# A decoder layer with state-space mixing, cross attention and experts: three residual sums moved into the accumulation of the products

## The chip, the cores and the metric

The kernel runs on one core of one Trainium2 chip. The metric is the device time of one execution in microseconds (us); the time of a kernel is the median of several executions. Five engines work side by side, each through its own queue in order: TensorE (PE, with its weight loads PEld), VectorE (DVE), ScalarE (ACT), GpSimd (POOL) and SyncE (SP), which here only issues transfers (DMA).

## The reference, cut to what matters

All arrays are float32: 32 batches of 256 rows of 256 columns. Each of the three parts adds its result to its input and normalizes each row.

```python
def _layernorm(x, axis=-1, eps=1e-05):
    m = jnp.mean(x, axis=axis, keepdims=True)
    v = jnp.var(x, axis=axis, keepdims=True)
    return (x - m) / jnp.sqrt(v + eps)
...
x = _layernorm(x + _L0_attn_ref(x, ...), axis=-1)        # state-space scan, ends in  y @ W_out.T + b_out
x = _layernorm(x + _L0_xattn_ref(x, ctx, ctx, ...), axis=-1)  # 16 heads, ends in  out @ w_o.T + b_o
x = _layernorm(x + _L0_ffn_ref(x, w1, w3, w2), axis=-1)  # 8 experts by position, (silu(x w1) * (x w3)) w2
return x
```

## The kernel before, in words

**Three streams of work run interleaved.** The first goes batch by batch through the state-space layer: projections, a short convolution, and then 512 scan steps in all, 16 for a batch. A step is a product `bu` on VectorE (L631), the scan itself on VectorE (L650, 128x1024), four exponentials on ScalarE that feed it (L602), and a multiplication of its result by C on GpSimd (L666). Every four steps PE sums over the states (`y`, L680) and VectorE gates the sum (`yg`, L696). The second stream is the attention of a batch: scores for the row maxima (`tops`, L897, on VectorE), scores again with exponentials on ScalarE (L955), and sums over the values (`ps_oT`, L924). The third is the experts: the rows of eight batches, regrouped by expert, are 32 units (`expert_unit`), each with three weight matrices loaded from memory. A unit computes two hidden products (`ps_h`, L1194), gates them on VectorE (L1258) and multiplies by w2 into one bank (`ps_down`, L1273). The last eight units hold two experts each, for four batches (the pair units), so that only four of them need the last batch.

**The three sums.** The product with `w_out` (name `ps_out`, in `mixes`), the product with `w_o` (`ps_o`, in `finish`) and `ps_down` each fill one PSUM bank of 128x512 float32, two halves of 128x256. VectorE adds the residual rows from SBUF (L823, L1025, L1285) and writes the sum over them in SBUF (`x1` or `xe`; the profile calls `x1` `x`). Then `layernorm` (L338) takes that SBUF tile: for each half `bn_stats` and `bn_aggr` on VectorE (L344, L345), four operations on 128x2 numbers on GpSimd for the factor and the offset (L348 to L352), and for each half one ScalarE operation that scales and shifts the rows in place (L355). For `x1` of the first norm, b_out has been added to the rows on GpSimd before (L810), and b_o after the norm (L837). 96 such norms run: 32 for each of the three places. The second stores its rows to `x2d` in memory, from where the experts load them again (`xe<-x2d`).

**PSUM.** Two pools: one for `b_bc` and `bu` of the scan, and a ring of five banks (`RING`, tag `mm`) that all other products share. A chain asks for banks with `take(n, rank, t)`, and gives one back with `done(n, t)` after the instruction that reads it last. The units ask with the lowest rank.

**What sets the order.** The order of instructions on every engine is fixed when the program is built. `Clock` keeps an assumed time for each engine, `spend` advances it by an assumed cost (`MM`, `VE`, `EV`, `GP`), and `in_order` always advances the chain (a generator) that can start first, with a lag per chain as its preference. Chains wait for each other through these assumed times only; on the chip each engine then runs its list in order and waits for its operands. A changed cost or a changed hold of a bank therefore changes the order on all engines, far from the changed lines. The units take what the other chains leave; those that haven't found a place before the scans end are done behind them.

Of the kernel before, what the change touches and what calls it, by code (L numbers as in the profile page):

```python
# [10 lines left out]
AF = mybir.ActivationFunctionType  # L11
ALU = mybir.AluOpType
# [4 lines left out]
P = 128  # L17
B, L, D = 32, 256, 256
DI, NS, DTR = 512, 16, 64
NDC = DI // P  # L20
# [19 lines left out]
NFC = 6  # L40
# [8 lines left out]
class Clock:  # L49
# [7 lines left out]
    def spend(self, engine, us, after=0.0):  # L57

        self.at[engine] = max(self.at[engine], after, self.base) + us
        return self.at[engine] + 0.3  # L60
# [40 lines left out]
def decoder_kernel(ctx: ExitStack, tc: tile.TileContext, a: dict, out: bass.AP):  # L101
    nc = tc.nc
    clock = Clock()
    spend = clock.spend
# [9 lines left out]
    ident = cpool.tile([P, P], F32, name="ident")  # L114
# [39 lines left out]
    def weight(name, rows, cols):  # L154
        t = wp.tile([P, rows // P, cols], F32, tag=name, name=name)
        dma(t, a[name].rearrange("(k p) c -> p k c", p=P))
        return t
# [72 lines left out]
    w_out = weight("w_out", DI, D)  # L230
    w_q, b_q = heads("q", "oT")
    w_o = weight("w_o", D, D)
# [16 lines left out]
    for i in range(3):  # L249
        t = keep.tile([P, GB, NQ, L], F32, name=f"da_{i}")  # L250
# [77 lines left out]
    def bank(name):  # L328
        return ps_mm.tile([P, 2 * L], F32, tag="mm", name=name)


    MM = 0.49
    EV = {1: 0.42, 2: 0.56, 4: 1.05}
    VE = {1: 0.41, 2: 0.66, 4: 1.225}
    CV = 0.535
    GP = {1: 0.7, 2: 1.23, 4: 2.36}

    def layernorm(tiles, t):  # L338

        n = len(tiles)  # L340
        mv = small.tile([P, n, 2], F32, tag="ln_mv", name="ln_mv")
        for i, x in enumerate(tiles):
            st = small.tile([P, 6], F32, tag="ln_st", name="ln_st")
            nc.vector.bn_stats(st, x)  # L344
            nc.vector.bn_aggr(mv[:, i, :], st)  # L345
        yield spend("DVE", 0.6 * n, t), "POOL"
        rstd = small.tile([P, n, 1], F32, tag="ln_rstd", name="ln_rstd")
        nc.gpsimd.tensor_scalar_add(rstd, mv[:, :, 1:2], EPS)  # L348
        nc.gpsimd.tensor_tensor(rstd, rstd, power[:, :n, :], ALU.pow)
        off = small.tile([P, n, 1], F32, tag="ln_off", name="ln_off")  # L350
        nc.gpsimd.tensor_tensor(off, mv[:, :, 0:1], rstd, ALU.mult)
        nc.gpsimd.tensor_scalar_mul(off, off, -1.0)  # L352
        yield spend("POOL", 1.5), "ACT"
        for i, x in enumerate(tiles):
            nc.scalar.activation(  # L355
                x, x, AF.Identity, bias=off[:, i, :], scale=rstd[:, i, :]
            )
        return spend("ACT", 0.55 * n)

# [431 lines left out]
    def mixes():  # L791


        yield lambda: None if later else spread.get(0), "DVE"
        bv = unit1.tile([P, 2, P], F32, tag="x1T", name="bv")
        nc.vector.tensor_copy(bv, b_v.to_broadcast([P, 2, P]))
        yield from take(1, 1, spend("DVE", 0.3))
        ps = bank("ps_bv")
        for k in range(2):
            nc.tensor.matmul(ps[:, :D], bv[:, k, :], w_o[:, k, :], start=(k == 0), stop=(k == 1))  # L800
        yield spend("PE", 2 * MM), "DVE"
        nc.vector.tensor_tensor(b_o, ps[:, :D], b_o, ALU.add)
        done(1, spend("DVE", VE[1]))
        for b in range(B):
            if b >= 2:
                yield lambda: stored[b - 2] + 3.0 if len(stored) >= b - 1 else None, "SP"
            load_x1(b)
            yield clock.at["SP"] + LANDING, "POOL"
            x1 = x1s[b]
            nc.gpsimd.tensor_tensor(  # L810
                x1, x1, b_out.unsqueeze(1).to_broadcast([P, 2, D]), ALU.add
            )
            spend("POOL", GP[2])
            yield lambda: gated.get(b), "PE"
            yield from take(1, 1, gated[b])
            yg = ygs.pop(b)
            ps, t = product(
                "ps_out",
                lambda t: [yg[:, k, t * P : (t + 1) * P] for k in range(NDC)],
                lambda t: [w_out[:, k, :] for k in range(NDC)],  # L820
            )
            yield t, "DVE"
            nc.vector.tensor_tensor(x1, ps, x1, ALU.add)  # L823
            t = spend("DVE", VE[2])
            done(1, t)
            t = yield from layernorm([x1[:, t, :] for t in range(2)], t)
            yield lambda: None if x1Ts else t, "PE"
            yield from take(1, 2, t)
            ps, t = transposes(x1)
            yield t, "ACT"  # L830
            x1T = unit1.tile([P, 2, L], F32, tag="x1T", name=f"x1T_{b}")
            nc.scalar.copy(x1T, ps)
            t = spend("ACT", EV[2])
            done(1, t)
            x1Ts[b] = x1T, t
            yield t, "POOL"
            nc.gpsimd.tensor_tensor(x1, x1, b_o.unsqueeze(1).to_broadcast([P, 2, D]), ALU.add)  # L837
            spend("POOL", GP[2])
# [146 lines left out]
    def finish(b):  # L985
        att = unit1.tile([P, 2, H, DK], F32, tag="att", name=f"att_{b}")
        HH = H // 2
        for g2 in range(2):

            yield lambda: oSs[0][1] if oSs else None, "PE"  # L990
            yield from take(1, 2.5, oSs[0][1])
            oS = oSs[0][0]
            ps = bank("ps_oB").rearrange("p (t j n) -> p t j n", t=2, j=2)
            for n in range(2):
                for j in range(2):
                    nc.tensor.transpose(ps[:, n, j, :], oS[:, j, n * P : (n + 1) * P], ident)
            del oSs[0]
            yield spend("PE", 0.6), "DVE"
            o = ps.rearrange("p t g (j c) -> p t (g j) c", c=32)
            rec = small.tile([P, 2, HH, 1], F32, tag="rec", name="rec")  # L1000
            nc.vector.reciprocal(rec, o[:, :, :, DK : DK + 1])
            nc.vector.tensor_tensor(
                att[:, :, g2 * HH : (g2 + 1) * HH, :],
                o[:, :, :, :DK],
                rec.to_broadcast([P, 2, HH, DK]),
                ALU.mult,
            )
            t = spend("DVE", 0.7)
            done(1, t)
        x1 = ending.pop(0)  # L1010
        yield from take(1, 3, t)
        ps, t = transposes(att.rearrange("p t h d -> p t (h d)"))
        yield t, "ACT"
        aT = unit1.tile([P, 2, L], F32, tag="aT", name=f"aT_{b}")
        nc.scalar.copy(aT, ps)
        t = spend("ACT", EV[2])
        done(1, t)
        yield from take(1, 2.5, t)
        ps, t = product(
            "ps_o",  # L1020
            lambda t: [aT[:, k, t * P : (t + 1) * P] for k in range(2)],
            lambda t: [w_o[:, k, :] for k in range(2)],
        )
        yield t, "DVE"
        nc.vector.tensor_tensor(x1, ps, x1, ALU.add)  # L1025
        t = spend("DVE", VE[2])
        done(1, t)
        t = yield from layernorm([x1[:, t, :] for t in range(2)], t)
        yield t, "SP"
        dma(x2d[b].rearrange("(t p) d -> p t d", p=P), x1)  # L1030
        stored.append(t)
# [129 lines left out]
    def expert_unit(bufs, u):  # L1161
# [12 lines left out]
        xe = xes.pop(u)  # L1174
        yield from take(1, unit_rank, x_at[u])
        ps = bank("ps_xe").rearrange("p (k e n) -> p k e n", k=2, e=2)
# [40 lines left out]
        for b in range(3):  # L1217
            yield weights("w1", b), "PE"
            yield from take(1, unit_rank, max(tx, weights("w1", b)()))
            ps, t = hidden("w1", b)  # L1220
# [10 lines left out]
        def second():  # L1231
# [19 lines left out]
            for b in range(3):  # L1251
                yield weights("w3", b), "PE"
                yield from take(1, unit_rank, max(th[0] - 2, weights("w3", b)()))
                ps, t = hidden("w3", b)
# [8 lines left out]
            po = bank("ps_down").rearrange("p (e n) -> p e n", e=2)  # L1263
            for j in range(2):
                e = es[j]
                if j == 0 or pair:
                    yield lambda: max(ts, w_at[u, "w2", e]) if (u, "w2", e) in w_at else None, "PE"
                terms = [i for i in range(len(FS)) if FS[i][0] == e]
                for i in terms:
                    f = FS[i][1]  # L1270
                    m = min(P, FF - f * P)
                    cols = slice(0, P) if pair else slice(j * P, (j + 1) * P)
                    nc.tensor.matmul(  # L1273
                        po[:, j, :],
                        h[i // m_in][:m, i % m_in, cols],
                        w_tiles[u, "w2", e][f // 3][:m, f % 3, :],
                        start=(i == terms[0]),
                        stop=(i == terms[-1]),
                    )
                t = spend("PE", NFC * MM)  # L1280
                if j == 1 or pair:
                    bufs.free["w2"].append(t)
            bufs.sets.append((place, t))
            yield t, "DVE"
            nc.vector.tensor_tensor(xe, po, xe, ALU.add)  # L1285
            t = spend("DVE", VE[2])
            done(1, t)
            t = yield from layernorm([xe[:, j, :] for j in range(2)], t)
            yield t, "SP"
            for j in range(2):  # L1290
                dma(rows_of(out, u, j), xe[:, j, :])
# [111 lines left out]
```

## Time and profile before

| | |
|---|---|
| median of three runs | 2786.34 us (2783.25 to 2790.03) |
| profiled execution | 2777.42 us, its span 2775.7 us |
| busy: PE, DVE | 2354.4 us, 2381.9 us |
| busy: ACT, POOL | 2063.1 us, 1787.5 us |
| mean granted TensorE clock | 0.899 |
| L823, L1025, L1285 | 32 each, 682, 673 and 682 ns |
| L344 and L345 | 192 each, 411 and 182 ns |
| L355 (192) | 597 ns on `x`, 596 on `xe` |
| start of the last scan | 2587.8 us |
| start of the last DVE sum (L1285) | 2767.6 us |

The span reaches from the first to the last instruction. A group of the profile names the line, the engine, the operation, the tiles `out<-in` with their shapes, the count, the busy time and the mean length of one in ns, and then the idle time of the engine just before them with what ended it. A float32 product of 128x256 stands in the trace as two records. In the windows, PEclk is the granted TensorE clock as a share of full speed.

### The profile page before, as it was taken

The page shows a single profiled execution, that of the slowest core. Times are in us where ns is not written, and L with a number is a line of the kernel's source. Part 1 is how long each engine was busy: PE and PEld are TensorE (multiplying, and loading weights), DVE is VectorE, ACT ScalarE, POOL GpSimd, SP SyncE. Part 2 cuts the span into 40 slices and gives each one's busy share as a digit, 9 for nine tenths or more (in the row PEclk, how much of TensorE's full clock was granted, in tenths as well). Part 3 has the DMA queues.
Part 4 walks back from the last instruction along what each step waited for, and adds up shares of the span by engine and source line. Part 5 has one row for each costly group of instructions (what it writes and reads, how often), then busy time and mean ns, then how long its engine had stood idle before and what let it go on. Part 6 is the DMA issues. An engine that isn't in the chain of part 4 may idle for free. (4 is left out here: it accounts for less than half of the span.)

```text
span 2775.7 us, 47073 instructions
## 1 busy us (share of the span) xinstructions
PE 2354.4 (85%) x16004; PEld 1644.8 (59%) x16004; DVE 2381.9 (86%) x2413; ACT 2063.1 (74%) x4331; POOL 1787.5 (64%) x1408
## 2 busy tenths in 40 slices
PE   6688888887898988898888988888779988888988
PEld 4555555565566666566555666655456655555767
DVE  3988999999999998999998998899998999988422
ACT  7777777888778887878787877877778777765531
POOL 5877777777776766666765766666766666655200
PEclk8888898989899999999789999999888988988999
DMA  7877777787788778677676887677678766777745
GB/s 196 235 208 207 215 222 223 229 231 225 215 229 224 215 203 228 183 221 201 185 198 176 233 221 199 192 203 194 178 197 218 206 201 192 199 207 215 221 148 176
DMA packets 403396, 573.93 MB, mean 207 GB/s; under 512 B 49300, under 2 KB 234900, under 8 KB 403156
## 3 DMA queue, kind: packets, MB, share of 16 engines
q1 hardware_dynamic: 403156, 570.92, 72.9%
q8 instruction: 127, 2.08, 0.3%
q14 instruction: 113, 0.93, 0.1%
HBM read 476.92 MB, written 93.85 MB: 206 GB/s over the span
## 5 line engine op out<-in xcount | busy, mean ns | idle before, releaser
L666 POOL TENSOR_TENSOR h<-h,c_bc 128x1024 f32<-128x1024 f32 x512 | 1209.9, 2364 | 555.6 <-DVE h L650 459.7
L650 DVE TENSOR_TENSOR_SCAN h<-da,bu 128x1024 f32<-128x1024 f32 x512 | 1168.6, 2282 | 45.1 <-ACT da L602 1.8
L602 ACT ACTIVATE da<-ld,a_neg 128x252 f32<-128x252 f32 x2048 | 865.4, 502 | 209.0 <-DVE h L650 135.6
L631 DVE TENSOR_TENSOR bu<-ld,b_bc 128x1024 f32<-128x1024 f32 x512 | 626.2, 1223 | 23.5 <-DMA ld<-dd 8.2
L1194 PE MATMUL ps_h<-x2T,w 128*128 128x256 f32 (+3 forms) x1632 | 390.9, 388 | 22.1 <-DVE x L1025 6.2
L955 ACT ACTIVATE es<-s 128x512 f32<-128x512 f32 x512 | 277.5, 594 | 175.9 <-PE ps_oT L924 101.1
L897 DVE TENSOR_REDUCE tops<-s 128x2 f32<-128x512 f32 x512 | 323.3, 678 | 65.8 <-PE s L865 65.7
L1194 PEld LDWEIGHTS ps_h<-x2T,w 128*128 128x128 f32 (+1 forms) x1632 | 278.0, 199 | 106.0 <-issue 28.2
L680 PE MATMUL y<-h,sel_y 128*32 128x256 f32 x4096 | 298.6, 414 | 37.6 <-POOL h L666 29.3
L374 PE MATMUL ps_in<-xT,w_in 128*128 128x256 f32 x1024 | 285.2, 429 | 43.3 <-ACT xT L414 33.6
L865 PE MATMUL s<-kT,qT 64*128 64x256 f32 x1024 | 184.8, 378 | 123.3 <-DVE tops L897 57.7
L374 PEld LDWEIGHTS ps_in<-xT,w_in 128*128 128x128 f32 x1024 | 209.6, 213 | 96.2 <-ACT xT L414 41.1
L865 PEld LDWEIGHTS s<-kT,qT 64*128 64x128 f32 x1024 | 114.7, 219 | 211.5 <-DVE tops L897 87.0
L680 PEld LDWEIGHTS y<-h,sel_y 128*32 128x32 f32 x4096 | 138.7, 117 | 164.1 <-POOL h L666 49.0
L865 PE MATMUL s<-qT,kT 64*128 64x256 f32 x1024 | 195.7, 345 | 31.9 <-DVE tops L897 11.7
L865 PEld LDWEIGHTS s<-qT,kT 64*128 64x128 f32 x1024 | 128.6, 206 | 102.4 <-issue 31.4
L449 POOL TENSOR_TENSOR u<-u,shifted 128x512 f32<-128x512 f32 x128 | 151.4, 1183 | 37.0 <-ACT u L436 31.8
L924 PE MATMUL ps_oT<-es,v 128*32 128x256 f32 x2048 | 163.1, 422 | 9.5 <-DVE tops L897 4.7
L875 PE MATMUL s<-mT,pick 64*128 64x256 f32 x1024 | 167.0, 308 | 3.4 <-ACT mT L914 3.4
L436 ACT ACTIVATE shifted<-ps_in,tap_b,conv_w 128x256 f32<-128x256 f32 x256 | 130.6, 565 | 29.6 <-PE ps_in L374 26.5
L348 POOL TENSOR_SCALAR ln_rstd<-ln_mv 128x2 f32<-128x2 f32 x96 | 21.2, 221 | 168.2 <-DVE ln_mv L345 163.2
L875 PEld LDWEIGHTS s<-mT,pick 64*128 64x128 f32 x1024 | 124.8, 209 | 4.0 <-ACT mT L914 3.6
(144 smaller groups left out, 3401.6 us busy)
## 6 DMA issues: line engine op xcount, KB each, us to landing
ld<-dd SPq DMA_DIRECT2D x1024, 256.0 KB, 4.1
w<-in_w SPq DMA_DIRECT2D x136, 352.0 KB, 5.0
kT<-k_all SPq DMA_DIRECT2D x256, 128.0 KB, 3.9
qT<-heads SPq DMA_DIRECT2D x128, 256.0 KB, 6.2
x<-in_x SPq DMA_DIRECT2D x64, 256.0 KB, 4.4
dd<-delta SPq DMA_DIRECT2D x32, 512.0 KB, 4.9
dd<-u SPq DMA_DIRECT2D x32, 512.0 KB, 5.1
w<-in_w SPq DMA_DIRECT2D x34, 384.0 KB, 4.2
```

Source lines behind the costliest of these rows:

```text
L374: nc.tensor.matmul(ps[:, j, :], l, r, start=(k == 0), stop=(k == len(terms) - 1))
L602: nc.scalar.activation(da[:, g, q].rearrange("p (k t) -> p k t", t=CHUNK)[:, :, 1:], loads[i][:, 0, g].rearrange("p (k t) -> p k t", t=CHU ...
L631: nc.vector.tensor_tensor(bu, loads[i][:, 1].unsqueeze(2).to_broadcast([P, GB, NQ, L]), b_bc.unsqueeze(1).to_broadcast([P, GB, NQ, L]), AL ...
L650: nc.vector.tensor_tensor_scan(h.rearrange("p g q t -> p (g q t)"), das_of.pop(i).rearrange("p g q t -> p (g q t)"), bu.rearrange("p g q t ...
L666: nc.gpsimd.tensor_tensor(hs[i], hs[i], c_bc, ALU.mult)
L680: nc.tensor.matmul(y[32 * j : 32 * j + 32, :], sel_y[:, g, :], hs[i - NJ + 1 + j][:, g, q, :], start=(g == 0 and q == 0), stop=(g == GB - ...
L865: nc.tensor.matmul(s[:, t, :], left[r : r + HR, g, t * P : (t + 1) * P], right[r : r + HR, g, :], start=True, stop=not lowered,)
L875: nc.tensor.matmul(s[:, t, :], pick[r : r + HR, g : g + 1].to_broadcast([HR, P]), mTs[g // NG][r : r + HR, :], start=False, stop=True,)
L897: nc.vector.tensor_reduce(top[:, h % 2, h // 2, :], s, AX.X, ALU.max)
L924: nc.tensor.matmul(oT[32 * j : 32 * j + 32, :], v[:, k, (4 * g + j) * DV : (4 * g + j) * DV + 32], ess[j][:, k, :], start=(k == 0), stop=( ...
L955: nc.scalar.activation(es, s, AF.Exp, scale=1.0 / DK**0.5)
L1194: nc.tensor.matmul(ps[:m, i, :], w_tiles[u, which, e][k][:, f * P : f * P + m], right, start=(k == 0), stop=(k == 1),)
```

## The change

Each of the three banks is started with one more product for each half: the identity as the stationary operand, the residual rows as the moving one. The bank then holds the sum. The VectorE sums are gone; `layernorm` reads its statistics and its rows from the bank, ScalarE writes the normalized rows to the same SBUF tile as before, and the bank is given back after the ScalarE rows instead of after the sum. In the planner's assumed costs the sums are dropped and a unit's last product is longer by one `MM`; the longer hold of the bank reaches it through `done`.

```diff
-    def layernorm(tiles, t):
+    def layernorm(tiles, outs, t):
...
-        for i, x in enumerate(tiles):
+        for i, (x, o) in enumerate(zip(tiles, outs)):
             nc.scalar.activation(
-                x, x, AF.Identity, bias=off[:, i, :], scale=rstd[:, i, :]
+                o, x, AF.Identity, bias=off[:, i, :], scale=rstd[:, i, :]
             )
...
             ps, t = product(
                 "ps_out",
-                lambda t: [yg[:, k, t * P : (t + 1) * P] for k in range(NDC)],
-                lambda t: [w_out[:, k, :] for k in range(NDC)],
+                lambda t: [ident] + [yg[:, k, t * P : (t + 1) * P] for k in range(NDC)],
+                lambda t: [x1[:, t, :]] + [w_out[:, k, :] for k in range(NDC)],
             )
             yield t, "DVE"
-            nc.vector.tensor_tensor(x1, ps, x1, ALU.add)
-            t = spend("DVE", VE[2])
+            halves = [x1[:, t, :] for t in range(2)]
+            t = yield from layernorm([ps[:, t, :] for t in range(2)], halves, t)
             done(1, t)
-            t = yield from layernorm([x1[:, t, :] for t in range(2)], t)
...
         ps, t = product(
             "ps_o",
-            lambda t: [aT[:, k, t * P : (t + 1) * P] for k in range(2)],
-            lambda t: [w_o[:, k, :] for k in range(2)],
+            lambda t: [ident] + [aT[:, k, t * P : (t + 1) * P] for k in range(2)],
+            lambda t: [x1[:, t, :]] + [w_o[:, k, :] for k in range(2)],
         )
         yield t, "DVE"
-        nc.vector.tensor_tensor(x1, ps, x1, ALU.add)
-        t = spend("DVE", VE[2])
+        halves = [x1[:, t, :] for t in range(2)]
+        t = yield from layernorm([ps[:, t, :] for t in range(2)], halves, t)
         done(1, t)
-        t = yield from layernorm([x1[:, t, :] for t in range(2)], t)
...
+                nc.tensor.matmul(po[:, j, :], ident, xe[:, j, :], start=True, stop=False)
                 for i in terms:
...
-                        start=(i == terms[0]),
+                        start=False,
                         stop=(i == terms[-1]),
                     )
-                t = spend("PE", NFC * MM)
+                t = spend("PE", (NFC + 1) * MM)
...
-            nc.vector.tensor_tensor(xe, po, xe, ALU.add)
-            t = spend("DVE", VE[2])
+            halves = [xe[:, j, :] for j in range(2)]
+            t = yield from layernorm([po[:, j, :] for j in range(2)], halves, t)
             done(1, t)
-            t = yield from layernorm([xe[:, j, :] for j in range(2)], t)
```

## The prediction

> **What bounds the kernel now.** I read the page first, then busy time by window, then VectorE's groups in the window that counts, then the end of the chain, and last the order in which the changed program, as built, issues its instructions on each engine.
>
> The page: a total per engine, and its share of each of 40 slices in tenths.
> ```profile
> PE 2354.4 (85%) x16004; PEld 1644.8 (59%) x16004; DVE 2381.9 (86%) x2413; ACT 2063.1 (74%) x4331; POOL 1787.5 (64%) x1408
> ...
> PE   6688888887898988898888988888779988888988
> ...
> DVE  3988999999999998999998998899998999988422
> ```
> VectorE (DVE) and TensorE (PE) look alike in the total and are not alike in time: DVE is at 9 until slice 37, then falls to 2, while PE goes on. The windows give the border. The last scan (L650) starts at 2587.8 us, the last y sum on PE ends at 2594.5.
> ```profile
> core 0: us, PE busy (x) PEld busy (x) DVE busy (x) ACT busy (x) POOL busy (x), PEclk, DMA share, GB/s
> 2594.50:2681.00 86.50, 80.25 (x573) 62.90 (x572) 27.28 (x61) 38.70 (x71) 10.70 (x27) 0.98 0.76 233
> 2681.00:2775.70 94.70, 74.20 (x496) 63.57 (x496) 17.38 (x41) 16.33 (x31) 6.73 (x20) 0.92 0.45 148
> 118.00:2590.00 2472.00, 2120.51 (x14517) 1461.32 (x14515) 2266.67 (x2257) 1917.18 (x4054) 1694.06 (x1286) 0.90 0.74 208
> ```
> So there are two stages. In the **middle** DVE works 92% of the time and PE 86%. In the **tail** (181.2 us after the last y sum) PE sets the end and DVE idles. What fills DVE in the middle:
> ```profile
> L650 DVE TENSOR_TENSOR_SCAN h<-da,bu 128x1024 f32<-128x1024 f32 x495 | 1129.7, 2282 | 42.5 <-ACT da L602 1.5 <-DVE bu L631 1.0 <-ACT oS L973 0.5
> L631 DVE TENSOR_TENSOR bu<-ld,b_bc 128x1024 f32<-128x1024 f32 x494 | 604.1, 1223 | 14.8 <-PE b_bc L572 6.0
> L897 DVE TENSOR_REDUCE tops<-s 128x2 f32<-128x512 f32 x496 | 313.1, 678 | 65.4 <-PE s L865 65.2
> ...
> L823 DVE TENSOR_TENSOR x<-ps_out,x 128x512 f32<-128x512 f32 x31 | 21.1, 681 | 3.3 <-PE ps_out L374 3.3
> L1025 DVE TENSOR_TENSOR x<-ps_o,x 128x512 f32<-128x512 f32 x30 | 20.1, 671 | 4.8 <-PE ps_o L374 4.6
> ...
> L1285 DVE TENSOR_TENSOR xe<-ps_down,xe 128x512 f32<-128x512 f32 x25 | 17.0, 680 | 10.8 <-PE ps_down L1273 10.8
> ```
> The reader is to see that scan and bu are three quarters of it and back to back, and that the three sums to be removed are 58 us here.
>
> **The middle, step by step.** Summing mean durations over DVE's issued instructions, from the 17th scan to the last: before 2375.5 us (in 2478.7 us of trace; records overlap by some 0.1 us), after 2298.7. The difference of 76.7 is 85 sums x 0.68 = 57.8, and 19 of other work that is only moved: the order has 24 of the 32 expert units done before the last scan now and 20 after the change, so their gating products and statistics (0.68 and 0.41 us each) wait for the tail. Batches without expert units (such as 269.1 to 346.4 us) have 73.6 us of DVE durations in a period of 77.3, those with one some 79 in 82: the gap is about 3 us either way, so I let time follow DVE's sum.
>
> The added work on PE in the middle is hidden by that bound: 1979 us of products at tail rates before the last y sum now, 1963 after, since the units that leave take more with them than the identity products bring. The identity product itself is one 128x256 fp32 product, like those of ps_down in the chain that ended last (start, us, what):
> ```profile
> 2685.79 2.14 DMA x2d<-x
> 2689.85 2.60 DMA xe<-x2d
> ...
> 2718.65 2.79 PE ps_down L1273 x12
> ...
> 2738.56 11.36 PE ps_h L1194 x96
> ```
> The trace holds two records for each fp32 product, so 12 are 6 products: 0.465 us each; the 128x128 products of ps_h take 11.36 / 48 = 0.237. 192 x 0.465 = 89 us more on PE in all. Its second operand is ready: x + b_out (L810) ends 14 us or more before ps_out starts in every batch.
>
> **New waits.** The bank was free after the sum, 0.68 us. Now it is held to the end of the two ScalarE rows; between the same two points the trace has 5.2 us (ps_out), 7.1 (ps_o), 5.5 (ps_down), medians. Over 31, 30 and 20 norms in the middle that is 428 us more of one of five banks, and the statistics start two products (0.93 us) later. Queued behind a PE instruction that waits for a bank are the y sums and scores, and DVE waits for those. Bounds: nothing, or 428 / 5 = 86 us if all five banks were always wanted. DVE's waits for PE in this window are about 136 us of 2472, 5.5%; I charge that share of the 86 and of 82 x 0.93 and round to 10. [...]
>
> **Statistics and rows from PSUM.** No bn_stats from PSUM is in the trace. The nearest rows, of VectorE and of ScalarE (mean ns after the comma):
> ```profile
> L344 DVE BATCH_NORM_STATS2 ln_st<-x 128x6 f32<-128x256 f32 x128 | 52.6, 411 | 2.2
> ...
> L585 DVE TENSOR_REDUCE a_neg<-a_all 128x64 f32<-128x512 f32 x1 | 0.7, 686 | 0.0
> ```
> ```profile
> L436 ACT ACTIVATE shifted<-ps_in,tap_b,conv_w 128x256 f32<-128x256 f32 x256 | 130.6, 565 | 29.6 <-PE ps_in L374 26.5
> ...
> L355 ACT ACTIVATE x<-x,ln_off,ln_rstd 128x256 f32<-128x256 f32 x128 | 70.0, 597 | 38.5 <-POOL ln_off L352 38.3
> ```
> A reduction over 512 elements takes 686 ns from SBUF and 678 from PSUM (L897 above), a multiplication of 128x1024 1226 (L521) and 1223: I take 0 for 162 statistics, from -8 ns (-1) to +13 ns (+2 us; att, a 128x256 operation that reads PSUM, is 424). ScalarE's row with two operands is 565 from PSUM against 597: 192 x 32 = 6 us less on an engine that bounds nothing, so 0. [...]
>
> So the middle: -76.7 + 10 = **-67**.
>
> **The tail.** The order has, after the last y sum, 612 products before and 928 after: of 128x256 in ps_down, ps_h, ps_out, ps_o, ps_qk (64 rows included) 104 and 274; of 128x128 in ps_h 312 and 384; scores 104 and 136; the rest transposes and ps_oT. At 0.465, 0.237, 0.116 and 0.13 that is 146.3 and 251.6 us. Four more units fall into it, and 14 identity pairs. The trace's 181.2 us are these 146.3, 18.3 of PE waits, 8.1 after the last product, and 8.5 left, so products run 6% dearer than my prices. After: 251.6 x 1.06 = 266.7. The largest wait, 9.6 us from the last ps_o over the store of x2d to the load of xe (chain above), has work to cover it: 500 products follow the last ps_o instead of 256, those of eight units, four of which don't need it. That leaves 8 of the waits, and 7.4 at the end without the sum: 282, **+101**. Bounds: +82 if products run at my prices and 4 us of waits go too; +125 if weights don't keep up: eight of these units load 4.2 MB each for 18.4 us of products, 230 GB/s, where 2594.5 to 2681 moved 233 at a share of 0.76.
>
> **Sum.** -67 + 101 = +34 us. The profiled execution took 2777.4 (span 2775.7 and 1.7 around it); it becomes 2811. The median of the runs is 8.9 higher; there I predict 2786.3 + 34 = **2820 us**. About 0.2% (5.6 us) is what a measurement can tell.
>
> **Rivals.**
> (1) Faster: the middle gains more than the tail costs, because DVE's waits for PE shrink as well. Of those 136 us, 65.2 stand at tops, and PE has 16 us less to do before the last y sum. Decides from: 24 us less of those waits than today, in place of the 10 more that I charge (-101 + 101 = 0). At 55 less: -132 + 101 = -31, 2755. Against it: batches without units, where PE is busy for 66 us and not 69 to 72, have the same 3 us gap.
> (2) The middle doesn't shorten: banks held five times longer make PE the bound, and DVE waits where it worked. For it: PE's weight loads waited 110.6 us for tops to free banks. Decides from 77 us of new waits: 2786 + 101 = 2887.
> (3) It evens out: -85 in the middle, +85 in the tail, 2786.
>
> **Chances.** Forecast (middle -45 to -87, tail +82 to +125, and of their sums those from +5.6 to +80: 2792 to 2866) 0.72; (1) 0.13; (2) 0.08; (3) 0.07. Faster 0.13, same 0.07, slower 0.80. The range 2772 to 2866 leaves out most of (2) and half of (1).
>
> **What would show it.** L823, L1025, L1285 gone from DVE; statistics near 0.41 us; rows near 0.565; the last scan near 2520 us instead of 2588; twelve expert norms after it; PE busy through a tail of about 280 us. I am wrong if the last scan comes after 2555 (banks or PE bound the middle) or before 2490, or if the tail stays under 250.

## The result, and the profile after

The changed kernel is slower: 2805.7 us, median of six runs, against 2780.3 for the kernel before, of six as well; the ratio is 1.0089 with a 95% interval of 1.0065 to 1.0113, so +25 us. The profiled execution took 2811.3 us, its span 2809.6, which is 33.9 more than the profiled span of before. The profiled execution is the longest of the six here, that of before lies below the median of its kernel, so the two profiles lie further apart than the medians.

The page after: totals, then the busy tenths of PE and of DVE in 40 slices.
```profile
PE 2426.6 (86%) x16388; PEld 1700.6 (61%) x16388; DVE 2317.8 (82%) x2317; ACT 2046.1 (73%) x4323; POOL 1787.8 (64%) x1408
...
PE   6788888888889898888889889888998888899998
...
DVE  3999989999998889999979989899999878993211
```
DVE lost 64 us and PE gained 72. VectorE's fall now begins one slice earlier and PE is at 9 longer behind it. In the windows of the changed kernel the border between the two stages is the last y sum, which ends at 2543.3 us (2594.5 before); the last scan starts at 2534.4.
```profile
core 0: us, PE busy (x) PEld busy (x) DVE busy (x) ACT busy (x) POOL busy (x), PEclk, DMA share, GB/s
118.00:2536.00 2418.00, 2087.59 (x14322) 1435.23 (x14320) 2190.68 (x2129) 1866.97 (x3982) 1687.82 (x1268) 0.91 0.74 206
2543.30:2658.00 114.70, 112.39 (x677) 82.79 (x678) 27.66 (x65) 51.49 (x97) 12.15 (x31) 0.97 0.46 142
2658.00:2809.60 151.60, 142.84 (x967) 123.10 (x965) 26.53 (x67) 36.24 (x68) 12.17 (x36) 0.98 0.63 208
```
The last y sum ends 51 us earlier. The tail is 266.3 us instead of 181.2, with PE busy for 255 of it: +85. VectorE's groups in the middle, of the changed kernel, where the three sums stood:
```profile
L650 DVE TENSOR_TENSOR_SCAN h<-da,bu 128x1024 f32<-128x1024 f32 x495 | 1130.0, 2283 | 44.7 <-ACT da L602 3.1
L631 DVE TENSOR_TENSOR bu<-ld,b_bc 128x1024 f32<-128x1024 f32 x494 | 604.3, 1223 | 18.7 <-PE b_bc L572 10.0 <-PE ps_m L911 0.4
L896 DVE TENSOR_REDUCE tops<-s 128x2 f32<-128x512 f32 x492 | 313.1, 678 | 68.9 <-PE s L864 68.8
...
L344 DVE BATCH_NORM_STATS2 ln_st<-ps_out 128x6 f32<-128x256 f32 x62 | 25.2, 407 | 6.5 <-PE ps_out L374 6.5
L344 DVE BATCH_NORM_STATS2 ln_st<-ps_o 128x6 f32<-128x256 f32 x60 | 24.5, 408 | 13.8 <-PE ps_o L374 13.8
L344 DVE BATCH_NORM_STATS2 ln_st<-ps_down 128x6 f32<-128x256 f32 x40 | 16.4, 410 | 20.6 <-PE ps_down L1272 20.5
```
The statistics cost no more from PSUM (407 to 410 ns) than from SBUF (411). What grew is the wait before them: 40.8 us for the three products, where the three sums waited 18.7. The same waits by number, and one of PE (who waited, for what: us in total, times, longest):
```profile
DVE ln_st L344 <- PE ps_down L1272: 20.5, 3, 8.1
DVE ln_st L344 <- PE ps_o L374: 13.8, 7, 3.9
DVE ln_st L344 <- PE ps_out L374: 6.5, 1, 6.5
PE ps_out L374 <- POOL x L810: 5.4, 1, 5.4
```
So these are eleven waits, where the sums had sixteen (at most 6.5 us each), and they are longer.

### The profile page after: what moved, and what is told of

The parts are those of the page before. It is cut to its first block, busy times and chain, and to the rows that moved or that the text cites. A ratio compares the mean times of both kernels' runs of the same rounds, so it can differ in the third digit from the quotient of the medians.

```text
span 2809.6 us, 47669 instructions
## 1 busy us (share of the span) xinstructions
PE 2426.6 (86%) x16388; PEld 1700.6 (61%) x16388; DVE 2317.8 (82%) x2317; ACT 2046.1 (73%) x4323; POOL 1787.8 (64%) x1408
## 4 chain that ended last, share of the span: by engine, by line
PE 32%; DVE 31%; ACT 12%; DMA 10%; issue 8%; POOL 4%; SPq 3%; DVEq 0%; ACTq 0%; POOLq 0%
DVE h L650 16%; PE ps_h L1192 8%; DVE bu L631 7%; ACT da L602 6%; DVE tops L896 5%; DMA ld<-dd 4%; PE s L864 4%; PE ps_down L1272 3%; PE y L680 3%; SPq L108 3%; DMA qT<-heads 2%; PE ps_oT L923 2%; PE ps_in L374 2%; POOL h L666 2%; PE ps_qk L374 2%
## 5 line engine op out<-in xcount | busy, mean ns | idle before, releaser
L1192 PE MATMUL ps_h<-x2T,w 128*128 128x256 f32 (+3 forms) x1440 | 334.2, 377 | 8.0 <-DVE att L1001 2.0
L1192 PEld LDWEIGHTS ps_h<-x2T,w 128*128 128x128 f32 (+1 forms) x1440 | 234.3, 190 | 78.3 <-issue 31.9
L374 PE MATMUL ps_in<-xT,w_in 128*128 128x256 f32 x1024 | 264.0, 404 | 15.6 <-DVE yg L696 5.5
L374 PEld LDWEIGHTS ps_in<-xT,w_in 128*128 128x128 f32 x1024 | 196.4, 200 | 63.1 <-issue 12.5
L864 PEld LDWEIGHTS s<-kT,qT 64*128 64x128 f32 x1024 | 108.2, 214 | 207.6 <-issue 76.5
L449 POOL TENSOR_TENSOR u<-u,shifted 128x512 f32<-128x512 f32 x128 | 151.6, 1185 | 30.0 <-ACT u L436 24.9
L923 PE MATMUL ps_oT<-es,v 128*32 128x256 f32 x2048 | 157.1, 416 | 6.1 <-DVE tops L896 3.6
L374 PE MATMUL ps_out<-w_out,yg 128*128 128x256 f32 x512 | 123.0, 384 | 0.0
```

The source lines that it names most:

```text
L374: nc.tensor.matmul(ps[:, j, :], l, r, start=(k == 0), stop=(k == len(terms) - 1))
L864: nc.tensor.matmul(s[:, t, :], left[r : r + HR, g, t * P : (t + 1) * P], right[r : r + HR, g, :], start=True, stop=not lowered,)
L923: nc.tensor.matmul(oT[32 * j : 32 * j + 32, :], v[:, k, (4 * g + j) * DV : (4 * g + j) * DV + 32], ess[j][:, k, :], start=(k == 0), stop=( ...
L1192: nc.tensor.matmul(ps[:m, i, :], w_tiles[u, which, e][k][:, f * P : f * P + m], right, start=(k == 0), stop=(k == 1),)
```

## The experiments

Each run is compared with the kernel before on the same chip in the same rounds (those runs lie between 2771.7 and 2802.0 us in all). A profile is one execution, so a border in it may be some us off. Differences in us are the ratio's share of 2780. "Middle" is the start of the last scan, "tail" the time from the start of the last record of the y sums to the end; before has 2587.8 and 181.6, the changed kernel 2534.4 and 266.7.

| run | ratio (95%) | middle | tail |
|---|---|---|---|
| the change | 1.0089 (1.0065 to 1.0113) | 2534.4 | 266.7 |
| e1 hold in the plan only | 1.0030 (1.0003 to 1.0057) | 2599.5 | 189.3 |
| e2 products, sums kept | 1.0046 (1.0024 to 1.0069) | 2578.0 | 214.1 |
| e3 no sums, no products | 0.9838 (0.9791 to 0.9885) | 2538.9 | 188.4 |
| e4 the units alone | 0.9925 (0.9895 to 0.9955) | 2557.8 | 192.2 |
| e5 bank copied out at once | 0.9927 (0.9900 to 0.9954) | 2540.7 | 215.9 |
| e6 the two norms alone | 0.9989 (0.9961 to 1.0018) | 2547.1 | 225.4 |
| e7 the change, units ranked first | 1.0328 (1.0270 to 1.0386) | 2652.6 | 226.1 |
| e8 before, units ranked first | 1.0131 (1.0075 to 1.0187) | 2619.6 | 200.6 |
| e9 e5 with the long hold in the plan | 1.0140 (1.0108 to 1.0172) | 2514.7 | 292.8 |
| e10 e5, tail sums on VectorE | 0.9911 (0.9887 to 0.9936) | 2534.3 | 211.2 |
| e11 e5 for the two norms alone | 0.9929 (0.9903 to 0.9956) | 2557.8 | 194.7 |

### e1: the hold alone

```diff
             nc.vector.tensor_tensor(x1, ps, x1, ALU.add)
             t = spend("DVE", VE[2])
-            done(1, t)
             t = yield from layernorm([x1[:, t, :] for t in range(2)], t)
+            done(1, t)
```
(and the same for `ps_o` and `ps_down`)

> The kernel before; only the planner is told that the three banks come back after the norm's ScalarE rows instead of after the sum (the instructions themselves are those of before, so on the chip nothing is held longer). Theory (PE's supply of time sets the tail, DVE's sum the middle): the new order has the same 2375.5 us of DVE work up to the last scan and 153 instead of 147 us of products after the last y sum, so +6 us, ratio 1.000 to 1.004. Rival (the longer hold makes the plan worse and that is the loss): most of the 25 us, +18 or more, ratio 1.006 or above.

Ratio 1.0030, inside what the theory gave. By itself, with the sums still on VectorE, the longer hold in the plan costs some 8 us. This spoke against the hold as the cause; e9 below limits that to a kernel without the identity products.

### e2: the products alone

```diff
-                lambda t: [yg[:, k, t * P : (t + 1) * P] for k in range(NDC)],
-                lambda t: [w_out[:, k, :] for k in range(NDC)],
+                lambda t: [ident] + [yg[:, k, t * P : (t + 1) * P] for k in range(NDC)],
+                lambda t: [x1[:, t, :]] + [w_out[:, k, :] for k in range(NDC)],
...
             nc.vector.tensor_tensor(x1, ps, x1, ALU.add)
```

> The kernel before with the 192 identity products added and nothing taken away: the VectorE sums stay, so the residual is counted twice, and the banks come back after the sums. Theory: DVE's work up to the last scan hardly changes (2371.5 us), 179 instead of 147 us of products stand after the last y sum, and the sums start two products later: +28 us and 10 to 20 of new DVE waits, so +38 to +48, ratio 1.014 to 1.017, slower than the changed kernel. Rival (the bank's hold is the loss, the products hide beside VectorE): within 5 us of before.

Measured 1.0046, +13 us: neither. The two stages of this run:
```profile
118.00:2578.00 2460.00, 2136.33 (x14694) 1476.98 (x14692) 2261.10 (x2247) 1911.06 (x4039) 1693.17 (x1282) 0.92 0.74 207
2584.50:2798.60 214.10, 186.06 (x1276) 154.51 (x1268) 49.07 (x110) 63.55 (x118) 19.57 (x54) 0.95 0.58 187
```
The tail grew by 32.5 us, as counted. The middle did not grow by the expected waits, it shrank by 10, though PE had some 57 us more of products in it (by the order, 89 more in all and 32 more in the tail). So the middle had room on PE, and the products by themselves are not the 25 us.

### e3: neither sums nor products

```diff
-                lambda t: [ident] + [yg[:, k, t * P : (t + 1) * P] for k in range(NDC)],
-                lambda t: [x1[:, t, :]] + [w_out[:, k, :] for k in range(NDC)],
+                lambda t: [yg[:, k, t * P : (t + 1) * P] for k in range(NDC)],
+                lambda t: [w_out[:, k, :] for k in range(NDC)],
...
-                nc.tensor.matmul(po[:, j, :], ident, xe[:, j, :], start=True, stop=False)
```

> The changed kernel without the identity products: no sums and no products, the residual is left out; statistics and rows still from the bank, which is held as long as in the changed kernel. Theory: DVE's work up to the last scan 2314.9 us (-61), products after the last y sum 168 us (+20), few new waits: -30 to -41 us, ratio 0.985 to 0.989. Rival (hold): the hold is all there, so not faster than before, +10 to +25 us. Rival (statistics and rows from PSUM cost): the same sign as the hold.

Ratio 0.9838, -45 us, a little beyond the theory's range and far from both rivals. Taking the sums from VectorE is worth its count, with statistics and rows from the bank and with the bank held to the end. From here to the changed kernel the only step is the 192 products, and it costs 70 us; from before to e2 the same products cost 13. The parts don't add up, and that asked for another theory. Nor does a shorter middle with the long hold send units to the tail by itself: e3 has both, and 24 units have their statistics before its last scan, as in the kernel before; the changed kernel has 20.

### e4 and e6: one place at a time

e4 keeps the VectorE sums of `ps_out` and `ps_o`, e6 those of `ps_down`:
```diff
-                nc.tensor.matmul(po[:, j, :], ident, xe[:, j, :], start=True, stop=False)
...
-            halves = [xe[:, j, :] for j in range(2)]
-            t = yield from layernorm([po[:, j, :] for j in range(2)], halves, t)
+            nc.vector.tensor_tensor(xe, po, xe, ALU.add)
+            t = spend("DVE", VE[2])
             done(1, t)
+            t = yield from layernorm([xe[:, j, :] for j in range(2)], [xe[:, j, :] for j in range(2)], t)
```
(this is e6; e4 does the same to `ps_out` and `ps_o`)

> The change for the expert units alone (32 of the 96 norms); ps_out and ps_o keep their VectorE sums. Theory: DVE's work up to the last scan 2359.2 us (-16), products after the last y sum 159 us (+12), new waits 3 to 8 us: -5 to +5 us, no difference. Rival (hold: a third of the norms, a third of the loss): +8 us. If the tail's identity products (8 units, 7.4 us) weigh more than counted, +10.

> The change for the two norms of the batch (ps_out, ps_o) alone; the expert units keep their VectorE sums. It is what is left of the change when the units' part is taken away. Both theories: DVE's work up to the last scan 2320.4 us (-55), products after the last y sum 210 us (+63), so +8 us, and up to 10 of new waits, +8 to +18. If the parts simply added up (units alone measured -21 us, the whole +25) it would be +46.

e4 measured 0.9925 (-21 us), better than expected; e6 0.9989, no difference, where +8 to +18 was expected. The sum of the two parts would be -24 us; the whole is +25. In e4 the tail is as counted (+11), and the middle gained 30 instead of the 16 us of its sums.

### e5 and e9: the bank, and the plan's view of it

Theory A was the one of the prediction: a shorter middle gives PE less time, so units must go to the tail, whatever the banks do. Theory B: PE has the time, but the plan lets the norms keep banks, and the units, which ask with the lowest rank, are not given any. e5 leaves all work of the change on VectorE and PE and shortens the hold:
```diff
-            yield t, "DVE"
+            yield t, "ACT"
+            nc.scalar.copy(x1, ps)
+            t = spend("ACT", EV[2], t)
+            done(1, t)
+            yield t, "DVE"
             halves = [x1[:, t, :] for t in range(2)]
-            t = yield from layernorm([ps[:, t, :] for t in range(2)], halves, t)
-            done(1, t)
+            t = yield from layernorm(halves, halves, t)
```
(and the same for `ps_o` and `ps_down`)

> The changed kernel (identity products, no VectorE sums), but ScalarE first copies the finished bank to SBUF and the bank comes back after that copy; statistics and rows are taken from SBUF. So the same VectorE and PE work as in the changed kernel, 96 copies more on ScalarE, and a bank held about as long as in the kernel before. Theory A (PE's supply of time in a shorter middle, whatever the banks): as the changed kernel, +15 to +29 us against before. Theory B (the plan starves the expert units of banks while the norms hold them, and so sends them to the tail): the order has 196 us of products after the last y sum instead of 252, and DVE's work up to the last scan is 2311.5 us; -64 + 49 = -15 us, with up to 10 of new waits -15 to -5.

e9 is e5 with `done(1, t)` moved behind `layernorm`, as in e1; the instructions of the three places are those of e5.

> The kernel of e5_copy (identity products, ScalarE copies the bank, statistics and rows from SBUF), with the planner told that the bank comes back only after the norm's ScalarE rows. On the chip the bank is still read last by the copy. If the changed kernel loses through its plan (banks counted as taken, so the expert units wait), this kernel loses too: the order has 2296.9 us of DVE work up to the last scan (-79) and 274 us of products after the last y sum (+128), so +49 us, with new waits +35 to +65. If it loses because banks are really held on the chip, this kernel stays near e5_copy, -20 to -5.

Ratios 0.9927 and 1.0140: -20 and +39 us. Busy times of both, the middle and the tail of each; first e5, then e9:
```profile
118.00:2540.70 2422.70, 2103.46 (x14628) 1462.07 (x14628) 2205.38 (x2159) 1929.22 (x4112) 1694.11 (x1280) 0.92 0.76 209
2547.00:2762.90 215.90, 199.69 (x1375) 165.60 (x1372) 44.05 (x106) 75.06 (x140) 20.19 (x55) 0.97 0.60 192
```
```profile
118.00:2514.70 2396.70, 2054.03 (x14236) 1414.92 (x14234) 2189.75 (x2121) 1903.35 (x4048) 1685.02 (x1263) 0.91 0.74 206
2524.90:2817.70 292.80, 277.78 (x1720) 222.52 (x1712) 57.42 (x139) 104.54 (x191) 26.34 (x74) 0.98 0.57 183
```
The statistics of the units before the last scan, two for a unit; e3, e5, e9:
```profile
L344 DVE BATCH_NORM_STATS2 ln_st<-ps_down 128x6 f32<-128x256 f32 x48 | 19.7, 411 | 9.0 <-PE ps_down L1271 9.0
L344 DVE BATCH_NORM_STATS2 ln_st<-xe 128x6 f32<-128x256 f32 x46 | 18.6, 404 | 12.8 <-ACT xe L1290 12.8
L344 DVE BATCH_NORM_STATS2 ln_st<-xe 128x6 f32<-128x256 f32 x36 | 14.6, 406 | 9.6 <-ACT xe L1290 9.6
```
The reader is to see the PE records before the last scan: 14628 in e5, 14321 in the changed kernel up to its own last scan (2534.4), in nearly the same time, and 23 units done against 20. PE had room for 300 records more, and the plan did not use it. So theory A falls. e9 differs from e5 by the plan alone: told of the long hold, it has only 18 units done before the last scan and 292.8 us of tail, though on the chip each bank is free after a copy. With the identity products in the kernel, the hold as the planner counts it sends units to the tail, as theory B says; without them it does not (e1 and e3, 24 units each).

The hold on the chip shows little in the changed kernel's own trace. PE was idle in its middle for 330 us (2418.0 - 2087.6), before for 351 (2472.0 - 2120.5). PE's waits there for a bank that a norm's ScalarE rows gave back come to 9.3 us, as far as the trace names the last releaser; before, those for a bank that a sum gave back come to 11.5. The longest group of each, before and after:
```profile
PE ps_h L1194 <- DVE x L1025: 6.2, 2, 3.1
```
```profile
PE ps_x L481 <- ACT x L355: 2.7, 1, 2.7
```

### e7 and e8: forcing the units forward

```diff
-        return 3 if len(gated) < 31 else 3.5
+        return 1.4 if len(gated) < 31 else 3.5
```
in the changed kernel (e7) and in the kernel before (e8); a smaller number asks first.

> The changed kernel, with one number of the plan changed: the expert units ask for banks at rank 1.4 instead of 3, ahead of scores and queries, as long as fewer than 31 batches are gated. The work is that of the changed kernel. The order has 26 units' gating products instead of 20 before the last scan, 173 instead of 252 us of products after the last y sum, and 2305.7 us of DVE work up to the last scan. Theory A: PE has no room for them in the middle, DVE waits instead, the last scan comes 30 us or more later than in the changed kernel and the time is 0 to +25 us against before. Theory B: PE has the room; -70 + 26 = -44 us, with 5 to 20 of new waits -39 to -24.

> The kernel before with the same rank of 1.4 for the units, to see what the rank does by itself. The order has 2366.1 us of DVE work up to the last scan (-9) and 149 us of products after the last y sum (+2). Both theories: -8 us, -15 to +5. If it gains as much as the changed kernel does with the rank, the rank and not the banks that the norms hold is what that run shows.

e7 measured 1.0328 (+91 us), e8 1.0131 (+36): both outside of all ranges. The order that looked best by its sums was the worst. The longest waits of VectorE in e7's middle:
```profile
DVE ln_st L344 <- PE ps_out L374: 66.8, 14, 11.2
DVE tops L896 <- PE s L864: 65.3, 51, 3.6
DVE ln_st L344 <- PE ps_down L1272: 33.1, 7, 6.3
DVE yg L696 <- PE y L680: 32.3, 27, 5.2
```
and one of PE:
```profile
PE ps_out L374 <- POOL x L810: 19.9, 12, 4.2
```
Statistics that stand in VectorE's list at their planned moment wait up to 11.2 us for `ps_out`, and the scans behind them come later: the last starts at 2652.6 us, in the changed kernel at 2534.4. In twelve batches the identity product itself waits for its operand, x + b_out from GpSimd; in e8 `ps_out` needs no such operand. As a test between A and B the pair decides nothing, since the rank does harm in the kernel before as well. It suggests that the count of DVE work plus tail products is good only between orders whose VectorE list keeps its products in time.

### e10 and e11: which version is best

e10 is e5, with this for units whose last product is issued after the last batch is gated:
```diff
+            late = len(gated) == B
...
+                if not late:
+                    nc.tensor.matmul(po[:, j, :], ident, xe[:, j, :], start=True, stop=False)
...
+            if late:
+                yield t, "DVE"
+                nc.vector.tensor_tensor(xe, po, xe, ALU.add)
+                t = spend("DVE", VE[2])
+            else:
+                yield t, "ACT"
+                nc.scalar.copy(xe, po)
+                t = spend("ACT", EV[2], t)
+            done(1, t)
```
e11 is e5 for `ps_out` and `ps_o` only; the units are those of before.

> e5_copy, but expert units whose last product is issued after the last batch is gated take their sum on VectorE as in the kernel before, without the identity products and the copy: in the tail PE sets the end and VectorE idles. The order is that of e5_copy up to the last scan (2311.5 us of DVE work), with 187 instead of 196 us of products after the last y sum. Expected 8 us below e5_copy: -23 to -31 us against before, ratio 0.989 to 0.992. If the tail isn't set by PE's products, no change against e5_copy (0.993).

> The copy and the identity products for the two norms of the batch alone; all expert units keep their VectorE sums. DVE's work up to the last scan 2329.3 us (-46), products after the last y sum 174 us (+27): -19 us, with what e5_copy had beside its sum (-5) -19 to -28, ratio 0.990 to 0.993. Against e6_norms (the same two norms with statistics and rows from the bank, ratio 0.999) it shows the hold alone.

e10 measured 0.9911 (2754.3 us), e11 0.9929 (2759.9), both inside the expectation. e11 against e6 shortens the hold, in the plan and on the chip, at the price of 64 ScalarE copies: 0.9929 against 0.9989, and the intervals do not overlap. Both beat the kernel before and the changed one; between e10, e11, e4 and e5 the intervals overlap, so none of them is shown to be the best.

## Why the prediction was right, and where it was not

It had the sign and the order of size: +34 us forecast, +25 by the runs, +33.9 in the profile. That the profile meets the forecast is luck: up to the last y sum it gained 51 us instead of 67, and the tail grew by 85 instead of 101, two errors of 16 in opposite directions. Point by point:

- **Two stages, VectorE's sum in the middle and PE in the tail: right.** The borders moved as forecast, the last scan to 2534.4 (forecast near 2520), the tail to 266.3 (forecast 282).
- **The sums' 58 us and the 19 of moved work: right as a count.** Summed over the traces, VectorE's operations from the 17th scan to the last take 2377.3 us before and 2301.0 after, 76.3 less where 76.7 was counted. The last scan moved by 53.4.
- **New waits, 10 us: the term that was mis-sized.** VectorE's waits for PE in the middle went from 142 (the prediction read 136) to 166 us, 24 more, and 22 of these stand where the sums were and the statistics are now (18.7 to 40.8). Products that end 0.93 us later do not explain them: they are eleven waits of up to 8.1 us. In the one for `ps_out` another step was wrong. "Its second operand is ready" was read from the order before; in the changed order x + b_out (L810) comes late for one batch, PE stands 5.4 us for it, and VectorE then waits 6.5 us for the product. In the others of over 0.5 us PE was at work for the whole wait; why the products came that late, no run shows.
- **The tail, +101: 16 too much.** PE was busy for 255.2 of the 266.3 us, 1.4% above the 251.6 at tail prices and not 6%; it waited for 3.6 and not 8, and 7.5 stood after the last product, as forecast. The granted clock was 0.97 and 0.98 in the two windows of this tail, 0.98 and 0.92 in those of before; that the clock made the surcharge is not shown.
- **The 9.6 us of waiting for the store of x2d: right.** After the last ps_o PE was busy for 142.8 of 151.6 us, and 7.5 of the rest stand after the last product.
- **Statistics and rows from PSUM: right.** 0.407 to 0.410 us against a forecast of 0.411, and the ScalarE rows:
```profile
L355 ACT ACTIVATE x<-ps_out,ln_off,ln_rstd 128x256 f32<-128x256 f32 x64 | 32.6, 563 | 7.9 <-POOL ln_off L352 7.7
```
  The ScalarE rows took 563 ns from PSUM here (forecast 565) against 597 from SBUF before.
- **Why the units move: not asked, and it is what matters.** The prediction read from the order that four units fall into the tail, and priced them. It sought the cost of the hold in waits on the chip, at most 86 us, charged at 5.5%. The runs show it in the plan: with the same work on VectorE and PE and a short hold (e5) the change gains 20 us, and with the long hold told to the plan alone (e9) it loses 39. "Since the units that leave take more with them" described an effect of the plan as if it followed from the work. Emptying the bank at once was worth it here (0.9927 in e5 against 1.0089), but the waits on the chip that the prediction drew from the 428 us do not show.
- **Rivals.** (1) did not come: the waits grew. (2) did not come as told; its banks are the cause, but through the order, and the middle did shorten. (3) had the tail right (+85), but the middle gave back 51 us and not 85.

What stays open: why the long hold in the plan sends units to the tail only beside the identity products. With the sums kept it costs 8 us (e1); with the shorter middle and neither sums nor products the kernel gains 45 all the same (e3); with the products and without the sums it costs 59 (e9 against e5). In the plan the products take time of PE, and they lengthen the time for which their own banks are taken; no run separates the two. Nor does any run have a sixth bank in the ring.

## What to carry to other kernels

Where a planner orders the work, price an edit twice: what its instructions cost on each engine, and what the resources it holds (a bank, a buffer) do to everybody who has to ask for them. The sum that moved to PE also brought PE the waits for its operand (for L810, 5.4 us here and 19.9 in e7). The accumulation in PSUM saved VectorE a sum of 0.67 to 0.68 us, and it turned a short-lived bank into a long-lived one where nothing emptied the bank at once; a ScalarE copy of 0.58 us (e5), on an engine busy for 73% of the changed kernel's span, paid for itself here. When the parts of a change don't add up (-21 and -3 us that make +25), look for a shared resource before a mispriced instruction.

## What the runs showed of the hardware

The granted clock of TensorE is not the same for all of these kernels: on the same chip its mean over the runs is 0.901 for the kernel before and 0.918 for e2, which has more products in nearly the same time. In e2 this went with a middle that was shorter by 10 us, not longer. Within the kernel before, runs with a lower clock are longer on the whole: 2771.7 us at 0.908, 2797.7 at 0.895, with exceptions such as 2796.3 at 0.902. PE was busy for 86.8% of e2's middle and for 85.8% of that of before. No run here changes the clock alone, so that it caused the 10 us is not shown.
